# A Softplus burst and a copy moved ahead of a pair of exponentials in a four-layer state-space kernel

## The chip, the cores and the metric

The kernel runs on one core of a Trainium2 chip. The core has five engines that work side by side, each through its own list of instructions in order: PE (matrix products), DVE (vector work), ACT (functions such as the exponential, each set of which needs a table to be loaded), POOL (general vector work) and SP, which here only starts DMA transfers. The metric is the device time of one execution in microseconds (us). Before the change it is 17365.62 us, the median of three runs (17365.36 to 17379.11).

## What is computed

Eight images of 48 x 48 positions and 96 channels go through four layers, each added to its input. Layers 0 and 3 are two-dimensional state-space layers, layer 2 is one along rows and columns, and layer 1 is a small network between an enlargement and a reduction of the image. The heart of layers 0, 2 and 3 is a scan over 2304 positions, for each of four directions, 192 channels and 16 states:

```python
delta = jax.nn.softplus(dts + dt_projs_bias.reshape(K, Din)[None, :, :, None])
...
def step(h, inp):
    u, dl, Bv, Cv = inp
    dA = jnp.exp(dl[..., None] * A)
    h = h * dA + (dl * u)[..., None] * Bv[:, :, None, :]
    y = jnp.einsum('bkdn,bkn->bkd', h, Cv)
    return (h, y)
```

`delta` is the step size, B and C are made from the input by a small matrix product.

## The kernel before

**Tiling.** A direction of an image is cut into five blocks of 480 or 384 positions (`BLKS`). A block has eight slots (`NG`), each holding two states for 96 channels, and two slots make a turn: four turns a block, 640 turns a layer, 1920 in all. The function `scans` runs the loop over turns for all three scan layers. Each turn has three scans on DVE, in three pairs of units of up to 484 columns.

**The work of a turn.** `make_da(t, pair)` (L327) lets ACT write two exponentials into a PSUM tile `ps_da`, of which there are two, so that a pair is made while the scan of another reads its own. `scan(t, pair)` (L335) is the scan on DVE, in place in the tile `dbu`. `make_dbu` (L303) prepares the products (delta u) B of later slots, in part on DVE, in part on POOL; for each slot a table says how many of its three units go to POOL. DVE reads B from PSUM, from a tile `ps_b`, of which there is one; `copy_b` (L284) fills it on ACT. `make_hc` (L341) multiplies by C on POOL, `reduce` (L361, L363) sums over states on PE, and `done` (L758) takes the sum out of PSUM on ACT.

**The order.** There is no automatic scheduler: the order in which the program text gives out instructions is the order on each engine. In a turn, ACT gets `make_da(t, 1)`, `make_da(t, 2)`, `copy_b` for slot at+3, then what `aside(at)` gives out, then `make_da(t+1, 0)`, `copy_b` for slot at+4 and `aside(at+1)`. DVE gets scan 0, products for slot at+2, scan 1, products for slot at+3, scan 2.

**Beside the turns.** `aside` (called twice a turn, once for each slot) takes finished results of the guest out of PSUM (`guest.settle()`; the guest is layer 1, which runs along with layers 0 and 2), starts loads, takes a step of side work such as convolution or normalisation for other images, and runs the steps that are due for a block two ahead (`run(at)`). Those steps, which `stage1` returns with the slot at which each is due, make B, C, delta and delta u of that block: two matrix products, copies, two additions of the bias (L711, due at slots 4 and 5), then `s6`, one Softplus over both halves of the 192 channels (L735, due at slot 6), then `du` on POOL (L503, due at slot 7), and the stores. Slot 6 is the first of the fourth turn of a block. Softplus and the exponential need different tables, so `s6` brings a table load ahead of it and one ahead of the next exponential. The row-and-column layer (`lines`) has its own `stage1`, with no step of this kind.

Of the kernel before, what the change touches and what calls it, by code (L numbers as in the profile page):

```python
# [101 lines left out]
def vss_stack_kernel(ctx: ExitStack, tc: tile.TileContext, i: dict, out: bass.AP):  # L102
# [120 lines left out]
    def scans(dirs, order, restart, on_pool, a, pools, ps, stage1, opening, done, side, tail, ahead=None, guest=None):  # L223
# [29 lines left out]
        def load_dd(b, half):  # L253

            t = pools["dd"].tile([P, 3 * 2 * WMAX], F32, tag="dd", name="dd")
            nc.sync.dma_start(t[:, :6 * b.m], b.dd[half].unsqueeze(1).to_broadcast([32, 4, 6 * b.m]))
            b.got[half] = t[:, :6 * b.m].rearrange("p (g t m) -> p g t m", g=3, t=2)

        def load_bc(t):

            b, slot = blocks[t // NG], t % NG
            sg = ORDER[slot][1]
            other = t - slot + NG - 1 - slot
            n = min(free, key=lambda n: free[n])
            free[n] = other
            r = bufs[n]
            rows4 = b.bcd[8 * sg:8 * sg + 8, :].rearrange("(s w) n -> s (w n)", w=2)
            nc.sync.dma_start(r[:, LEAD:LEAD + 2 * b.n], rows4.unsqueeze(0).to_broadcast([32, 4, 2 * b.n]))

            lo, hi = LEAD - b.at.start, LEAD + b.n  # L270
            bcs[t] = bcs[other] = r[:, lo:hi + b.at.start], r[:, hi:hi + b.n]

        def copy_b(t):

            if t >= NG * len(blocks):
                return
            b, slot = blocks[t // NG], t % NG
            if on_pool.get(slot) == 3:
                return
            if slot == NG // 2 and t - 1 in bps:  # L280
                bps[t] = bps[t - 1]
                return
            bps[t] = ps("b", 1)
            nc.scalar.copy(bps[t][:, :bcs[t][0].shape[1]], bcs[t][0])  # L284

        def units(tile, b, lo, hi):
            return tile[:, lo * b.m:hi * b.m].rearrange("p (u m) -> p u m", m=b.m)

        def make_dbu(t, engine):

            if t >= NG * len(blocks):
                return
            b, slot = blocks[t // NG], t % NG
            if t // 2 not in dbus:
                dbus[t // 2] = rooms[t // 2 % (NG // 2)]
            cut = 3 - on_pool.get(slot, 0)
            lo, hi = (0, cut) if engine is nc.vector else (cut, 3)
            if lo == hi:
                return
            o = units(dbus[t // 2], b, 3 * (slot % 2) + lo, 3 * (slot % 2) + hi)[:, :, b.by]  # L300
            du = b.got[ORDER[slot][0]][:, lo:hi, 1, b.by]
            by = (bps[t] if engine is nc.vector else bcs[t][0])[:, b.by]
            engine.tensor_mul(o, du, by.unsqueeze(1).to_broadcast([P, hi - lo, by.shape[1]]))  # L303
# [13 lines left out]
        def make_da(t, pair):  # L317
            if t >= nt:
                return
            b, q = turns[t]  # L320
            da = ps("da", 2, 1024)
            das[t, pair] = da
            for u in (2 * pair, 2 * pair + 1):
                half, sg = ORDER[2 * q + u // 3]
                ci = half * 12 + sg * 3 + u % 3
                at = (u - 2 * pair) * b.m
                nc.scalar.activation(da[:, at:at + b.m], b.got[half][:, u % 3, 0, :], AF.Exp, scale=a[:, b.k, ci:ci + 1])  # L327

        def scan(t, pair):
            b, q = turns[t]  # L330
            da = das.pop((t, pair))[:, :2 * b.m]
            db = dbus[t][:, 2 * pair * b.m:(2 * pair + 2) * b.m]
            if b.back:
                da, db = da[:, ::-1], db[:, ::-1]
            nc.vector.tensor_tensor_scan(db, da, db, 0.0, ALU.mult, ALU.add)  # L335

        def make_hc(t, sub):
            b, q = turns[t]
            n = b.n
            h = units(dbus[t], b, 3 * sub, 3 * sub + 3)[:, :, b.at]  # L340
            nc.gpsimd.tensor_mul(h, h, bcs.pop(2 * t + sub)[1].unsqueeze(1).to_broadcast([P, 3, n]))  # L341
# [24 lines left out]
            if sub == 1:  # L366
                dbus.pop(t)

        steps = {}

        def plan(b, at):
            b.got = {}
            sources(b, pools)
            for n, step in stage1(b).items():
                steps.setdefault(at + n, []).append(step)

        def run(t):
            for step in steps.pop(t, []):
                step()

        for n, b in enumerate(blocks[:3]):
            plan(b, NG * (n - 2))
        for t in range(-2 * NG - 1, 0):
            run(t)
            for _ in range(2):
                next(ahead, None)
            while tail:
                tail.pop(0)()
            if t == -NG:
                for n in range(4):  # L390
                    load_bc(n)
            if t == 2 - NG:
                for half in range(2):
                    load_dd(blocks[0], half)
# [30 lines left out]
        for t, (b, q) in enumerate(turns):  # L425
            at, nblk = 2 * t, t // (NG // 2)
            if q == 0:
                if nblk + 3 < len(blocks):
                    plan(blocks[nblk + 3], at + NG)
                if b.k == order[0] and b.first:  # L430
                    beside = side(b.job)
            scan(t, 0)
            if t > 0:
                make_hc(t - 1, 1)
            make_dbu(at + 2, nc.vector)
            make_da(t, 1)
            make_dbu(at + 2, nc.gpsimd)
            make_dbu(at + 3, nc.gpsimd)
            if t > 0:
                reduce(t - 1, 0)  # L440
            scan(t, 1)
            make_da(t, 2)
            copy_b(at + 3)
            make_dbu(at + 3, nc.vector)
            if t > 0:
                reduce(t - 1, 1)
            aside(at)
            begin(t + 2)
            make_hc(t, 0)
            make_da(t + 1, 0)  # L450
            scan(t, 2)
            copy_b(at + 4)
            finish(at + 1)
            aside(at + 1)
            if q == NG // 2 - 1 and b.k == order[-1] and b.last:
                for _ in beside:
                    while tail:
                        tail.pop(0)()
# [25 lines left out]
    def sources(b, pools):  # L484
        b.dd = [pools["dr"].tile([32, 6 * b.m], F32, tag=f"dd{half}_{b.n}", name=f"dd{half}") for half in range(2)]
        b.bcd = pools["dr"].tile([2 * NS, b.n], F32, tag=f"bcd_{b.n}", name="bcd")
# [4 lines left out]
    def sizes(b, half):  # L491

        return [b.dds[:, half, n, b.at] for n in range(2)]
# [20 lines left out]
    def ss2d(l, xin, xout, guest=None):  # L514
# [15 lines left out]
        for n in ("in", "xp", "out"):  # L530
            of = i[f"{l}_{n}"]
# [168 lines left out]
        def stage1(b):  # L700
            n = b.n
            u, uall = b.view(us[b.job], dirs[b.k][0]), b.view(uss[b.job], dirs[b.k][0])
            got = {}

            def raw(half):
                got["p"] = ps("s1", 1)
                nc.tensor.matmul(got["p"][:, :n], lhsT=wide("dtw", (2 * b.k + half) * DH), rhs=b.bcl[:, :n],  # L707
                                 start=True, stop=True)

            def biased(half):  # L710
                nc.scalar.activation(sizes(b, half)[0], got["p"][:DH, :n], AF.Identity,  # L711
                                     bias=w[f"{l}_dtb"][:, b.k, half:half + 1])

            def s0():
                got["p"] = ps("s1", 1)
                for half in range(2):
                    nc.tensor.matmul(got["p"][:, :n], lhsT=wide("xp", (2 * b.k + half) * NBC), rhs=uall[:, half],  # L717
                                     start=(half == 0), stop=(half == 1))

            def s1():  # L720
                b.bcl = pools["bcl"]
                nc.scalar.copy(b.bcl[:NBC, :n], got["p"][:NBC, :n])

            def s3():
                nc.sync.dma_start(b.bcd, b.bcl[:2 * NS, :n])
                raw(0)

            def s4():
                make_room(b, pools)
                biased(0)  # L730
                raw(1)

            def s6():
                both = b.dds[:, :, 0, b.at]
                nc.scalar.activation(both, both, AF.Softplus)  # L735

            def du():
                make_du(b, u)

            def store(half):  # L740
                return lambda: store_dd(b, half)

            return {-1: s0, 1: s1, 3: s3, 4: s4, 5: lambda: biased(1), 6: s6, 7: du,
                    NG: store(0), NG + 1: store(1)}

        def so_far(b, half):
# [606 lines left out]
```

## Time and profile before

| | |
|---|---|
| median of three runs | 17365.62 us |
| the profiled execution | 17373.84 us |
| its span, from first to last instruction | 17371.9 us |
| layer 0, scan loop | 115 to 5809 us |
| layer 2, scan loop | 5906 to 11826 us |
| layer 3, scan loop | 11948 to 17345 us |
| mean granted clock of PE | 0.843 of full speed |

The costliest groups of instructions, each with its line, engine, operation, tiles (written <- read), shape, count, then busy time in us and mean length of one in ns, and last the engine's idle time just before them, with what ended most of it:

```profile
L335 DVE TENSOR_TENSOR_SCAN dbu<-ps_da,dbu 128x968 f32<-128x968 f32 (+3 forms) x5760 | 11823.5, 2075 | 814.5 <-ACT ps_da L327 653.1
L341 POOL TENSOR_TENSOR dbu<-dbu,bc 128x1440 f32<-128x1440 f32 (+1 forms) x3840 | 10069.9, 2635 | 1775.7 <-DVE dbu L335 1715.3
L327 ACT ACTIVATE ps_da<-dd,w_l_a 128x484 f32<-128x484 f32 (+3 forms) x11520 | 7423.0, 649 | 2308.3 <-DVE dbu L335 2078.8
L303 DVE TENSOR_TENSOR dbu<-dd,ps_b 128x962 f32<-128x962 f32 (+5 forms) x2880 | 3831.0, 1330 | 286.1 <-ACT ps_b L284 157.3
L284 ACT COPY ps_b<-bc 128x482 f32<-128x482 f32 (+3 forms) x2720 | 1448.8, 533 | 227.1 <-DVE dbu L303 185.3
L327 ACT ACT_TABLE_LOAD x993 | 1274.0, 1283 | 17.5
```

Of Softplus alone there are 320, 1.01 us for a wide block and 0.85 us for a narrow one, each behind a table load of 1.28 us. In a timeline, a row that ends in x4 is four instructions merged; the bracket at the end of a row is idle time of the engine before it, and what ended it.

### The profile page before, as it was taken

The numbers are of one execution on the slowest core, as the hardware profiler recorded it, in microseconds if no ns is written. First come the engines' busy times: TensorE is split into PE (matmuls) and PEld (weight loads), VectorE is DVE, ScalarE is ACT, GpSimd is POOL, SyncE is SP. The second block draws the span as 40 slices with busy tenths as digits, with TensorE's granted clock in tenths as the row PEclk, the third lists the DMA queues.
The fourth block names the chain that finished last, engine by engine and source line by source line (L and its number), as shares of the span: only waits on it lengthen the run. The fifth ranks groups of instructions, "written<-read, shape, count | busy, mean of one in ns | idle before, by whom it ended". The sixth has DMA issues, their size and how long they took to land.

```text
span 17371.9 us, 169003 instructions
## 1 busy us (share of the span) xinstructions
PE 13193.7 (76%) x53740; PEld 4744.7 (27%) x53740; DVE 15807.2 (91%) x9840; ACT 13897.8 (80%) x20972; POOL 15212.7 (88%) x8159
## 2 busy tenths in 40 slices
PE   6778788878787677777777777776777777777776
PEld 1223232323232333233233322221222222222221
DVE  7999999998899789899889999996999999999998
ACT  6888888878787688888888888886878878878876
POOL 7998888988889788888888888887999999999998
PEclk7888888888897888899889988887878878878877
DMA  4555555454545344444444444443455555555454
GB/s 141 178 174 169 176 168 179 167 183 165 173 169 181 130 149 165 149 157 154 156 155 149 159 158 155 150 155 128 171 173 176 174 174 175 174 169 179 169 176 144
DMA packets 887919, 2843.67 MB, mean 164 GB/s; under 512 B 353468, under 2 KB 421788, under 8 KB 760206
## 3 DMA queue, kind: packets, MB, share of 16 engines
q1 hardware_dynamic: 887022, 2832.85, 48.0%
q8 instruction: 423, 6.93, 0.2%
q14 instruction: 474, 3.88, 0.1%
HBM read 2384.40 MB, written 448.17 MB: 163 GB/s over the span
## 4 chain that ended last, share of the span: by engine, by line
ACT 22%; DVE 21%; POOL 19%; issue 14%; PE 13%; DMA 10%; SPq 1%; POOLq 0%; DVEq 0%; ACTq 0%
DVE dbu L335 14%; POOL dbu L341 12%; ACT ps_da L327 8%; DVE dbu L303 6%; POOL dbu L303 4%; DMA dd<-dds 4%; DMA dd<-dd 3%; ACT L327 3%; PE ps_y L361 2%; POOL dds L503 2%; ACT ps_b L284 1%; PE ps_sa L944 1%; PE ps_sa L889 1%; DMA bc<-bcd 1%; ACT L907 1%
## 5 line engine op out<-in xcount | busy, mean ns | idle before, releaser
L335 DVE TENSOR_TENSOR_SCAN dbu<-ps_da,dbu 128x968 f32<-128x968 f32 (+3 forms) x5760 | 11823.5, 2075 | 814.5 <-ACT ps_da L327 653.1
L341 POOL TENSOR_TENSOR dbu<-dbu,bc 128x1440 f32<-128x1440 f32 (+1 forms) x3840 | 10069.9, 2635 | 1775.7 <-DVE dbu L335 1715.3
L327 ACT ACTIVATE ps_da<-dd,w_l_a 128x484 f32<-128x484 f32 (+3 forms) x11520 | 7423.0, 649 | 2308.3 <-DVE dbu L335 2078.8
L361 PE MATMUL ps_y<-dbu,w_red 128*32 128x480 f32 (+1 forms) x23040 | 4206.5, 651 | 1588.0 <-POOL dbu L341 1554.0
L363 PE MATMUL ps_y<-dbu,w_red 128*32 128x480 f32 (+1 forms) x7680 | 4168.0, 651 | 0.0
L303 DVE TENSOR_TENSOR dbu<-dd,ps_b 128x962 f32<-128x962 f32 (+5 forms) x2880 | 3831.0, 1330 | 286.1 <-ACT ps_b L284 157.3
L303 POOL TENSOR_TENSOR dbu<-dd,bc 128x481 f32<-128x481 f32 (+5 forms) x2240 | 3913.5, 1762 | 22.5 <-DMA dd<-dd 18.2
L361 PEld LDWEIGHTS ps_y<-dbu,w_red 128*32 128x32 f32 x23040 | 724.9, 118 | 5000.1 <-POOL dbu L341 3338.6
L284 ACT COPY ps_b<-bc 128x482 f32<-128x482 f32 (+3 forms) x2720 | 1448.8, 533 | 227.1 <-DVE dbu L303 185.3
L578 PE MATMUL ps_side<-xpad,w_l_cw 128*128 128x480 f32 (+1 forms) x2880 | 1360.4, 611 | 46.4 <-ACT g_room L1179 16.3
L327 ACT ACT_TABLE_LOAD x993 | 1274.0, 1283 | 17.5
L707 PE MATMUL ps_s<-bcl,square 128*128 128x480 f32 (+1 forms) x1280 | 890.0, 786 | 324.1 <-ACT dds L711 169.5
L357 PE MATMUL ps_y<-big,eye 128*128 128x480 f32 (+1 forms) x960 | 745.0, 865 | 243.5 <-ACT big L758 238.9
L717 PE MATMUL ps_s<-big,square 128*128 128x480 f32 (+1 forms) x1280 | 844.9, 790 | 66.1 <-ACT g_room L1179 18.4
L503 POOL TENSOR_TENSOR dds<-dds,big 96x960 f32<-96x960 f32 (+1 forms) x320 | 706.7, 2209 | 144.9 <-ACT dds L735 144.6
L578 PEld LDWEIGHTS ps_side<-xpad,w_l_cw 128*128 128x128 f32 x2880 | 575.0, 210 | 815.0 <-issue 703.4
L889 PE MATMUL ps_sa<-ub,square 128*128 128x480 f32 (+1 forms) x640 | 411.7, 782 | 394.2 <-ACT ub L879 394.2
L363 PEld LDWEIGHTS ps_y<-dbu,w_red 128*32 128x32 f32 x7680 | 661.9, 118 | 0.0
L870 PE MATMUL ps_sb<-xpad,square 128*128 128x480 f32 (+1 forms) x1280 | 595.2, 611 | 84.7 <-ACT g_room L1179 32.7
L870 PE MATMUL ps_sa<-xpad,square 128*128 128x480 f32 (+1 forms) x1280 | 537.9, 561 | 0.0
L711 ACT ACTIVATE dds<-ps_s,w_l_dtb 96x480 f32<-96x480 f32 (+1 forms) x640 | 405.1, 633 | 124.6 <-DMA dd<-dds 82.9
L758 ACT COPY big<-ps_y 96x480 f32<-96x480 f32 (+1 forms) x640 | 471.6, 737 | 38.7 <-PE ps_y L363 37.4
(244 smaller groups left out, 12498.7 us busy)
## 6 DMA issues: line engine op xcount, KB each, us to landing
dd<-dd SPq DMA_DIRECT2D x512, 1452.0 KB
bc<-bcd SPq DMA_DIRECT2D x1536, 480.0 KB
dd<-dd SPq DMA_DIRECT2D x256, 1440.0 KB
dd<-dds SPq DMA_DIRECT2D x512, 363.0 KB
dd<-dd SPq DMA_DIRECT2D x128, 1164.0 KB
bc<-bcd SPq DMA_DIRECT2D x384, 384.0 KB
dd<-dds SPq DMA_DIRECT2D x256, 360.0 KB
dd<-dd SPq DMA_DIRECT2D x64, 1152.0 KB
```

The costliest lines, as they stand in the source:

```text
L284: nc.scalar.copy(bps[t][:, :bcs[t][0].shape[1]], bcs[t][0])
L303: engine.tensor_mul(o, du, by.unsqueeze(1).to_broadcast([P, hi - lo, by.shape[1]]))
L327: nc.scalar.activation(da[:, at:at + b.m], b.got[half][:, u % 3, 0, :], AF.Exp, scale=a[:, b.k, ci:ci + 1])
L335: nc.vector.tensor_tensor_scan(db, da, db, 0.0, ALU.mult, ALU.add)
L341: nc.gpsimd.tensor_mul(h, h, bcs.pop(2 * t + sub)[1].unsqueeze(1).to_broadcast([P, 3, n]))
L361: nc.tensor.matmul(y[32 * g:32 * g + 32, :n], lhsT=wc["red"][:, :32], rhs=hc[:, g, b.at], start=False, stop=(slot == 3))
L363: nc.tensor.matmul(y[DH:, :n], lhsT=wc["red"][:, 32:], rhs=hc[:, 2, b.at], start=False, stop=(slot == 3))
L503: nc.gpsimd.tensor_mul(du, dt, u)
L578: nc.tensor.matmul(pu[:, :n], lhsT=flat[:, at:at + P], rhs=xpad[:, r0 + dy:r0 + dy + nr, dx:dx + W], start=(tap == 0), stop=(tap == 8))
L707: nc.tensor.matmul(got["p"][:, :n], lhsT=wide("dtw", (2 * b.k + half) * DH), rhs=b.bcl[:, :n], start=True, stop=True)
L717: nc.tensor.matmul(got["p"][:, :n], lhsT=wide("xp", (2 * b.k + half) * NBC), rhs=uall[:, half], start=(half == 0), stop=(half == 1))
L870: nc.tensor.matmul(got["u", half][:, :n], lhsT=wide("cw", at), rhs=shifted(off), start=(tap == 0), stop=(tap == 3))
```

## The change

Steps that `stage1` gives with a tuple as their slot go into a second list, `bursts`. In layers 0 and 3 this is `s6` alone, the Softplus. In the loop, the burst that is due at slot `at` is given out behind `make_da(t, 1)` and no longer in `aside(at)`, which comes behind `make_da(t, 2)` and the copy of B. Where there is a burst in the turn, `copy_b(at + 3)`, the copy for the odd slot, follows it at once, and so stands ahead of `make_da(t, 2)` too. In the other turns, and in layer 2, the order is as it was.

```diff
-        steps = {}
+        steps, bursts = {}, {}
 
         def plan(b, at):
             b.got = {}
             sources(b, pools)
             for n, step in stage1(b).items():
-                steps.setdefault(at + n, []).append(step)
-
-        def run(t):
-            for step in steps.pop(t, []):
+                if isinstance(n, tuple):
+                    bursts.setdefault(at + n[0], []).append(step)
+                else:
+                    steps.setdefault(at + n, []).append(step)
+
+        def run(t, of=steps):
+            for step in of.pop(t, []):
                 step()
...
         for t in range(-2 * NG - 1, 0):
+            run(t, bursts)
             run(t)
...
             make_dbu(at + 2, nc.vector)
             make_da(t, 1)
+            early = at in bursts
+            run(at, bursts)
+            if early:
+                copy_b(at + 3)
             make_dbu(at + 2, nc.gpsimd)
             make_dbu(at + 3, nc.gpsimd)
             if t > 0:
                 reduce(t - 1, 0)
             scan(t, 1)
             make_da(t, 2)
-            copy_b(at + 3)
+            if not early:
+                copy_b(at + 3)
             make_dbu(at + 3, nc.vector)
...
-            return {-1: s0, 1: s1, 3: s3, 4: s4, 5: lambda: biased(1), 6: s6, 7: du,
+            return {-1: s0, 1: s1, 3: s3, 4: s4, 5: lambda: biased(1), (6,): s6, 7: du,
                     NG: store(0), NG + 1: store(1)}
```

In layer 2's own `stage1` every due slot is a plain number, so nothing of it moves.

## The prediction, made before the result

> **Terms.** A turn handles two of a block's eight slots. In it E0, E1, E2 are the three pairs of exponentials on ACT (L327), S0, S1, S2 the three scans on DVE (L335) that consume them, D the products `make_dbu` (L303) that DVE makes between scans for the next turn. The burst is: load the Softplus table, Softplus (L735), and the load of the Exp table that the next exponential then needs. It stands in the fourth turn of a block; E0' and S0' belong to the turn after it.
>
> **What bounds the kernel now.** I read the busy shares first, then DVE's waits, then two stretches around a burst.
>
> ```profile
> span 17371.9 us, 169003 instructions
> PE 13193.7 (76%) x53740; PEld 4744.7 (27%) x53740; DVE 15807.2 (91%) x9840; ACT 13897.8 (80%) x20972; POOL 15212.7 (88%) x8159
> ```
>
> DVE is idle for 17371.9 - 15807.2 = 1565 us in all, so a change that only moves ACT work can win no more than a part of that. The waits of DVE name the part that ACT causes:
>
> ```profile
> DVE dbu L335 <- ACT ps_da L327: 653.1, 614, 4.5
> DVE dbu L335 <- issue: 94.5, 75, 4.5
> DVE dbu L335 <- POOL dbu L341: 28.3, 17, 1.9
> ```
>
> Scans wait 653 us for exponentials; POOL, though 88% busy, holds scans for 28 us only. The middle layer (5906 to 11826 us) has no L735 at all, so I sorted DVE's idle time in the two outer layers by turn and scan. Before S0', the scan behind a burst, it is 155 us in the first layer and 38 us in the last (158 bursts each); before S2 of the burst's turn it is 0.0 us in both. Those 193 us are all that the change can give back directly, and the zero is what it can spoil.
>
> The timeline of ACT in the last layer (start, length, engine, line, names):
>
> ```profile
> 14234.73 0.56 ACT L711 ACTIVATE dds<-ps_s,w_l_dtb 96x384 f32<-96x384 f32 x1
> 14235.19 2.65 ACT L327 ACTIVATE ps_da<-dd,w_l_a 128x484 f32<-128x484 f32 x4
> 14237.91 0.56 ACT L284 COPY ps_b<-bc 128x482 f32<-128x482 f32 x1
> 14238.50 1.28 ACT L735 ACT_TABLE_LOAD   x1
> 14239.79 0.85 ACT L735 ACTIVATE dds<-dds 96x768 f32<-96x768 f32 x1
> 14240.66 1.28 ACT L327 ACT_TABLE_LOAD   x1
> 14241.95 1.37 ACT L327 ACTIVATE ps_da<-dd,w_l_a 128x484 f32<-128x484 f32 x2
> ```
>
> and of DVE beside it:
>
> ```profile
> 14236.25 1.63 DVE L303 TENSOR_TENSOR dbu<-dd,ps_b 128x1443 f32<-128x1443 f32 x1
> 14237.80 2.16 DVE L335 TENSOR_TENSOR_SCAN dbu<-ps_da,dbu 128x968 f32<-128x968 f32 x1
> 14239.88 1.63 DVE L303 TENSOR_TENSOR dbu<-dd,ps_b 128x1443 f32<-128x1443 f32 x1
> 14241.43 4.23 DVE L335 TENSOR_TENSOR_SCAN dbu<-ps_da,dbu 128x968 f32<-128x968 f32 x2
> ```
>
> The reader should see two things. E1 and E2 are one run of four (x4): nothing on ACT waits between them, so there is no hole there for a burst. And S2 and S0' are one run of two (x2): behind the burst E0' ends at 14243.32, S2 ends about 14243.5, so here the burst is already hidden, narrowly, by S1, D and S2. In the first layer, evictions of the guest layer (L1172, L1190) stand ahead of the burst and the cover is gone:
>
> ```profile
> 2498.90 0.65 ACT L1172 ACTIVATE g_room<-ps_side,g_shift,g_rs 96x365 f32<-96x365 f32 x1
> 2501.30 0.40 ACT L1190 COPY g_room<-ps_s 73x288 f32<-73x288 f32 x1 [1.75 <-PE ps_s L1188]
> 2501.71 1.28 ACT L735 ACT_TABLE_LOAD   x1
> ```
> ```profile
> 2506.57 2.17 DVE L335 TENSOR_TENSOR_SCAN dbu<-ps_da,dbu 128x968 f32<-128x968 f32 x1 [2.79 <-ACT ps_da L327]
> ```
>
> **What the Trainium skill says.** "ScalarE: Activation LUTs", What ACT_TABLE_LOAD costs: a switch of table is a load of about 1283 ns and a drain of about 1380 ns. The trace agrees on the load (1283 ns, all 320 at L735) and not on the drain: the next ACTIVATE starts 0.01 us behind the load. I use 1.28 us. The same page, Table sets, says that copies and Identity are in every set; the trace agrees, L711 and L284 run between exponentials without a load. "Perfetto Trace Analysis", Identifying the Most-Contended Engine, ranks these engines by occupancy: DVE here. Its section on the DVE / Act instruction says that the update of a semaphore travels after the reported end; here S0' starts 0.03 us behind E0' where it waited (2505.17 + 1.37 to 2506.57), which is what I charge for a hand-over.
>
> **The change part by part.**
>
> *Instructions.* Nothing goes but line positions: the order on PE, DVE, POOL and SP is unchanged, and ACT has one table load more in the whole program (no Silu shares the burst's stretch, so no switch is saved or added). Cost of that: 1.3 us.
>
> *The burst ahead of E2.* ACT's order becomes E1, burst, copy of B, E2, evictions, E0'. The copy needs the previous D done, which it is before S1 starts, so it doesn't wait. From the end of E1 to the earliest S2, for the wide blocks: table 1.28, Softplus 1.01, copy 0.55, table 1.28, E2 1.37, gaps 0.08, hand-over 0.03, together 5.60 us. One block in five is narrow (Softplus 0.85, copy 0.47, or E2 1.20), so the mean is near 5.5. What covers it is the way from the end of E1 to S2 on DVE: rest of the wait for S1, S1 itself 2.16, D 1.63. Taken from the trace for the 158 turns of each layer, it is 4.35 us in the mean (median 4.2) in the first layer and 4.78 (median 4.8) in the last. So S2, never late before, becomes late by 5.5 - 4.35 = 1.15, about 1.2 us with the few turns of zero left out, and by 5.5 - 4.78 = 0.7, about 0.8 us. In the stretch above: E1 ends 14236.50, and 14236.50 + 1.28 + 0.85 + 0.56 + 1.28 + 1.37 + 0.11 = 14241.95 against 14241.43.
>
> *The copy put ahead too.* D for the odd slot reads it. It ends 2.88 us behind E1, S1 ends 2.2 to 3.3 us behind it, so D starts at most 0.7 us later, and ends 4.5 us behind E1, ahead of E2's 5.57. Hidden by E2; if E2 were not late this would cost 0.2 us a burst. Had the copy stayed behind E2, D would have started at 5.6 and S2 at 7.2.
>
> *The stall that goes.* ACT reaches E0' with the same work done, so E0' ends about when it did. S0' is then released by S2's end. Given back: 155 / 158 = 0.97 us a burst in the first layer, 38.5 / 158 = 0.24 in the last. What is late next is S2 itself, whose delay runs through to S0'.
>
> *Sum.* Last layer: 0.8 - 0.24 = +0.56 us, x 158 = +88 us. First layer: 1.2 - 0.97 = +0.23 us if E0' never is the later one. But in 100 of the 158 turns guest evictions stand between E2 and E0', and where such an eviction waits for PE, whose matmul waits for an eviction in front of it (the 1.75 us above), that wait moves along with E2 and E0' stays late; if it does in all, the net is +0.5. I take the middle, +0.37 x 158 = +58 us. In the turn behind, ACT has a little more room: the scans S1 there wait for ACT 16 + 5 us today, of which I take off 15. Together 88 + 58 - 15 + 1 = +132 us.
>
> *Does it stay?* ACT meets DVE again within two turns (in turn 1 of a block E0 waits for a scan in 132 and 156 of 156 blocks), so DVE's delay isn't won back there. POOL starts its second product of the burst's turn 1.65 us (median) behind S2 anyway, so S2's delay hardly reaches it. Softplus ends earlier, but its reader on POOL (L503) waits 31 us for it in the first layer and nothing in the last: nothing to win. SP's loads are far off.
>
> Against the profiled execution's 17373.84 us (8.2 above the median of 17365.62) this is 17506; against the median, **17497 us**, 0.8% slower.
>
> **Rivals.**
> 1. *Faster: the burst is hidden.* S2 isn't delayed because the cover is really as long as the burst, and S0' loses its stall. Speaks for it: S0' has the only systematic stall. Against: cover 4.35 and 4.78 against 5.5; only some 10% of turns have 5.6 or more. It decides if the chain behind E1 takes under 4.3 us in fact. It would give 17366 - 193 + 15 = about 17190; half of it, 17280.
> 2. *No change: exchange.* One stall for another of the same size, in the last layer taken up by waits for PE and POOL later on. For: both layers do the same work on ACT. Against: the last layer has only 38 us to give. 17366 +- 35.
> 3. *Slower by more.* Guest evictions come 3.5 us later against E1, so PE's next guest matmuls and the evictions behind them push E0' and the next turn's E1 as well, beyond the 1.2 us of room there (in the second stretch E1 of that turn ends at 2508.53, its S1 starts at 2509.71). At 0.5 us more for the 100 guest turns and the full +0.5 in the first layer: 132 + 50 + 21, and S2 late by another 0.1 in both, +32: about 17600.
> 4. *The text does not do what it says.* Excluded: all bursts of the loop are taken at E1, one per block.
>
> **How the numbers follow.** Forecast (17400 to 17570) 0.70, rival 3 (17570 and up) 0.12, rival 2 0.09, rival 1 0.09. Measurement can't tell changes under 0.2%, 35 us. The ends of the unknown sizes, first layer +0.1 to +0.5 and last +0.4 to +0.7, give +64 to +190, and with rival 3 the range is 17400 to 17590. Faster 0.09, within 0.2% 0.09, slower 0.82.
>
> **What would show it.** In the profile after, S2 of the burst's turn should wait for E2 (idle about 185 us in the first layer, 125 in the last), S0' should hardly wait in the last layer, DVE's wait for L327 should rise from 653 to about 653 + 310 - 137 = 826 us (137 is L327's share of the 193), and the table loads stay at 1283 ns. The forecast is wrong if S2 waits for under 0.4 us in the mean, or if DVE's idle time falls elsewhere.

## The result, and the profile after

The changed kernel takes 17445.32 us (median of 6 runs, 17421.44 to 17448.41), the kernel before 17368.66 us in the same comparison (6 runs, 17365.36 to 17384.28). The ratio is 1.0039, with a 95% interval of 1.0026 to 1.0052: about 77 us slower, where 132 us were forecast.

In the code after the change the lines of the steps are higher by 9: Softplus is L744 for L735, the bias L720 for L711, the guest's evictions L1181, L1188 and L1199 for L1172, L1179 and L1190. The busy time of each engine in the changed kernel:

```profile
PE 13221.8 (76%) x53740; PEld 4769.1 (27%) x53740; DVE 15826.8 (91%) x9840; ACT 13880.1 (80%) x20973; POOL 15217.0 (87%) x8159
```

No engine has more instructions of the kernel to do, but for one table load more on ACT. DVE's waits in the changed kernel, as who waited for whom, us in total, times, longest:

```profile
DVE dbu L335 <- ACT ps_da L327: 737.4, 800, 4.4
DVE dbu L303 <- ACT ps_b L284: 210.8, 106, 76.8
```

Scans waited for exponentials 614 times for 653 us before, now 800 times for 737 us: more often, and for less each time. The second line is new in the loops: before, a product D waited for its copy of B 6 times for 157 us (153 of them in two waits at the start of layers 0 and 3), now 106 times for 211 us.

The same turn of layer 3 that was shown before, on DVE and then on ACT (start, length, engine, line, operation, tiles, shape, count):

```profile
14289.60 2.16 DVE L335 TENSOR_TENSOR_SCAN dbu<-ps_da,dbu 128x968 f32<-128x968 f32 x1
14291.68 1.63 DVE L303 TENSOR_TENSOR dbu<-dd,ps_b 128x1443 f32<-128x1443 f32 x1
14293.68 4.24 DVE L335 TENSOR_TENSOR_SCAN dbu<-ps_da,dbu 128x968 f32<-128x968 f32 x2 [0.37 <-ACT ps_da L327]
```
```profile
14286.98 1.36 ACT L327 ACTIVATE ps_da<-dd,w_l_a 128x484 f32<-128x484 f32 x2
14288.36 1.28 ACT L744 ACT_TABLE_LOAD   x1
14289.66 0.85 ACT L744 ACTIVATE dds<-dds 96x768 f32<-96x768 f32 x1
14290.41 0.55 ACT L284 COPY ps_b<-bc 128x482 f32<-128x482 f32 x1
14290.98 1.28 ACT L327 ACT_TABLE_LOAD   x1
14292.27 2.66 ACT L327 ACTIVATE ps_da<-dd,w_l_a 128x484 f32<-128x484 f32 x4
```

The run of four exponentials is cut: E1 alone, then the burst and the copy, and then E2 and E0' as a new run of four. S2 now waits 0.37 us for E2; before, S2 followed D with no wait. S0' follows S2 at once, as it did before. So this turn only lost.

The turn of layer 0 that had a stall of 2.79 us at S0', on DVE and ACT after the change (two rows of ACT are left out):

```profile
2516.72 4.29 DVE L335 TENSOR_TENSOR_SCAN dbu<-ps_da,dbu 128x968 f32<-128x968 f32 x2 [0.82 <-ACT ps_da L327]
```
```profile
2515.32 1.37 ACT L327 ACTIVATE ps_da<-dd,w_l_a 128x484 f32<-128x484 f32 x2
2517.16 0.38 ACT L1199 COPY g_room<-ps_s 73x288 f32<-73x288 f32 x1
2517.44 1.37 ACT L327 ACTIVATE ps_da<-dd,w_l_a 128x484 f32<-128x484 f32 x2
2520.44 0.32 ACT L1199 COPY g_room<-ps_side 73x192 f32<-73x192 f32 x1 [1.15 <-PE ps_side L1197]
```

Here the change does what it can do: the stall of 2.79 us is gone, for one of 0.82 us at S2. The first eviction L1199 starts without a wait; its twin before the change waited 1.75 us for PE. But the second one, behind E0', now waits 1.15 us, ahead of the next turn's E1. Before the change it had no wait:

```profile
2506.96 0.31 ACT L1190 COPY g_room<-ps_side 73x192 f32<-73x192 f32 x1
```

Over all turns with a burst, taken from the two traces (157 turns a layer, means in us):

| | layer 0 before | after | layer 3 before | after |
|---|---|---|---|---|
| end of E1 to start of S2 | 4.34 | 5.49 | 4.76 | 5.49 |
| end of S2 to start of S0' | 1.23 | 0.20 | 0.47 | 0.16 |
| start of S1 to start of S0' | 6.95 | 7.09 | 6.17 | 6.59 |
| start of S1 to S1 of the next turn | 10.09 | 10.31 | 9.21 | 9.61 |
| from block to block | 35.51 | 35.75 | 33.62 | 33.84 |
| the layer's loop of scans | 5693.3 | 5736.9 | 5396.3 | 5429.0 |

The loops of layers 0 and 3 grew by 43.6 and 32.7 us; that of layer 2, in which nothing moved, shrank by 5.3 us. (It lies between 5898 and 5920 us in the profiles of all kernels here that leave layer 2 alone; what differs by 10 us in one layer of one profile is not told apart from that.)

### The profile page after: what moved, and what is told of

It is laid out like the page before. It is cut to its first block, busy times and chain, and to the rows that moved or that the text cites. A ratio compares the mean times of both kernels' runs of the same rounds, so it can differ in the third digit from the quotient of the medians.

```text
span 17443.4 us, 169089 instructions
## 1 busy us (share of the span) xinstructions
PE 13221.8 (76%) x53740; PEld 4769.1 (27%) x53740; DVE 15826.8 (91%) x9840; ACT 13880.1 (80%) x20973; POOL 15217.0 (87%) x8159
## 4 chain that ended last, share of the span: by engine, by line
ACT 24%; DVE 21%; POOL 15%; issue 14%; PE 13%; DMA 10%; SPq 1%; POOLq 0%; DVEq 0%; ACTq 0%
DVE dbu L335 14%; POOL dbu L341 9%; ACT ps_da L327 8%; DVE dbu L303 6%; DMA dd<-dds 4%; POOL dbu L303 4%; ACT L327 3%; DMA dd<-dd 3%; PE ps_y L361 2%; POOL dds L512 2%; ACT ps_b L284 2%; PE ps_sa L898 1%; DMA bc<-bcd 1%; PE ps_sa L953 1%; ACT L744 1%
## 5 line engine op out<-in xcount | busy, mean ns | idle before, releaser
L303 DVE TENSOR_TENSOR dbu<-dd,ps_b 128x962 f32<-128x962 f32 (+5 forms) x2880 | 3833.9, 1331 | 324.3 <-ACT ps_b L284 210.8
L303 POOL TENSOR_TENSOR dbu<-dd,bc 128x481 f32<-128x481 f32 (+5 forms) x2240 | 3913.9, 1762 | 22.4 <-DMA dd<-dd 18.8
L720 ACT ACTIVATE dds<-ps_s,w_l_dtb 96x480 f32<-96x480 f32 (+1 forms) x640 | 404.7, 632 | 108.7 <-DMA dd<-dds 69.3
```

## The experiments

Times before, in the same comparisons, are 17374.45 us for the first four, 17372.88 for the next three, 17369.63 for the last.

**One layer at a time.** The burst's slot is a tuple in one of the two layers only:

```diff
-            return {..., (6,): s6, 7: du,
+            return {..., (6,) if l == "l0" else 6: s6, 7: du,
```

> The new order in layer 0 only; layer 3 keeps the old one. Cover theory (the chain from the end of E1 over burst and copy to E2 is longer than what DVE has to do before S2; S2's delay less the stall given back at S0' is the loss): 158 x (1.14 - 1.00) = +22 us at the bursts, with what follows about +20 to +45 us. Rival (the loss comes about elsewhere, by guest evictions and PE that are later): all of the +77 us are here, since only this layer has a guest beside its bursts.

> The new order in layer 3 only. Cover theory: S2 later by 0.72 us, 0.31 given back at S0', 158 x 0.41 = +65 us, or the +33 us by which this layer's loop grew in the changed kernel if later waits for POOL and PE take part of it back. Rival (the loss is the guest's): 0 +- 15 us, there is no guest in this layer.

Layer 0 alone: 17407.73 us, ratio 1.0020 (1.0013 to 1.0027), +33 us. Layer 3 alone: 17410.02 us, 1.0019 (1.0012 to 1.0026), +36 us. Together that is +69 us against +77: the loss is in both layers and adds up. The guest can't be the cause of layer 3's half, since it isn't there. In layer 3 the +36 us are well under the +65 that the delay at S0' alone would give, so about half is taken back later.

Where it is taken back shows when the time from each scan to the next is summed over layer 3's loop, before and after the change. The way from S1 to S2 in the burst's turn grows by 113 us, that from S2 to S0' shrinks by 47, which leaves 66. Then the three turns between two bursts are shorter by 9, 13 and 9 us. With the change in layer 3 alone they are shorter by 8, 13 and 8 us, and with it in layer 0 alone none of them changes by much over 2 us. DVE's waits for POOL in layer 3's loop seem to name a cause. In the kernel before they are:

```profile
DVE dbu L335 <- POOL dbu L341: 21.3, 12, 1.9
DVE dbu L303 <- POOL dbu L315: 13.1, 10, 1.5
```

and all that is left of them in the changed one:

```profile
DVE dbu L303 <- POOL dbu L315: 1.0, 1, 1.0
```

But only the second group is gone: the product L303 in the second turn of a block waits 13 us for POOL before and 1.6 us after (waits too short for this view counted in), and that turn's 13 us are nearly all from there. The first group, scans of narrow blocks, still waits, under another name. One of these scans with its exponentials, before and after:

```profile
12467.37 1.21 ACT L327 ACTIVATE ps_da<-dd,w_l_a 128x388 f32<-128x388 f32 x2
12468.67 1.77 DVE L335 TENSOR_TENSOR_SCAN dbu<-ps_da,dbu 128x776 f32<-128x776 f32 x1 [1.84 <-POOL dbu L341]
```
```profile
12509.30 1.21 ACT L327 ACTIVATE ps_da<-dd,w_l_a 128x388 f32<-128x388 f32 x2
12510.60 1.77 DVE L335 TENSOR_TENSOR_SCAN dbu<-ps_da,dbu 128x776 f32<-128x776 f32 x1 [1.83 <-issue]
```

Both start 0.09 us behind the end of their exponentials, so both wait for ACT, and neither for what the bracket says. The same holds for all 14 such scans: 25.6 us before (21.3 put down to POOL, 4.3 to "issue"), 24.6 us after, all put down to "issue". So POOL accounts for 11 of the 31 us taken back; the rest are small waits, 7 us of them waits of the burst turn's own S0 for its exponentials. That DVE's delay is what makes these waits shorter is argued, not shown. It fits the next two experiments, in which layer 3's S0' is later still and the three turns together are shorter by 34 and 42 us.

**The burst moved, the copy left behind E2.**

```diff
             make_da(t, 1)
             early = at in bursts
             run(at, bursts)
-            if early:
-                copy_b(at + 3)
...
             make_da(t, 2)
-            if not early:
-                copy_b(at + 3)
+            copy_b(at + 3)
```

> Burst behind E1 as in the change, the copy of B back behind E2. Cover theory: the product D waits for the copy and S2 for D, so the chain from E1 is table 1.28, Softplus 1.0, table 1.28, E2 1.35, copy 0.53, D 1.6, about 7.1 us, against a cover of 4.35 and 4.78: S2 late by 2.7 and 2.3 us, less 1.0 and 0.3 given back, 158 x (1.7 + 2.0) = about +580 us over before. Rival (the copy was hidden either way, its move does nothing): +77 us like the change.

Measured: 17871.87 us, ratio 1.0284 (1.0269 to 1.0299), +497 us. The rival falls. S2 comes 7.10 and 7.08 us behind E1's end (expected about 7.1). In the profile of this kernel, layer 3's turn:

```profile
14592.15 1.66 DVE L303 TENSOR_TENSOR dbu<-dd,ps_b 128x1443 f32<-128x1443 f32 x1 [1.95 <-ACT ps_b L284]
14593.72 4.23 DVE L335 TENSOR_TENSOR_SCAN dbu<-ps_da,dbu 128x968 f32<-128x968 f32 x2
```
```profile
14590.26 1.37 ACT L327 ACTIVATE ps_da<-dd,w_l_a 128x484 f32<-128x484 f32 x2
14591.57 0.54 ACT L284 COPY ps_b<-bc 128x482 f32<-128x482 f32 x1
```

E2 is ready at 14591.63, but S2 can't use it: D stands ahead of S2 on DVE and waits for the copy until 14592.15. The move of the copy is the half of the change that keeps it cheap. Of the 83 us between 580 and 497, about 25 are missing at S0' already, which is late by 1.62 and 1.89 us in the mean (555 us in all); most of the rest is again recovered later, since a block is longer by 1.53 and 1.66 us.

**The copy ahead of the burst.** The two are exchanged:

```diff
             early = at in bursts
-            run(at, bursts)
             if early:
                 copy_b(at + 3)
+            run(at, bursts)
```

> E1, copy, burst, E2: the copy ahead of the burst and not behind it. Cover theory: the copy has one PSUM tile and waits until DVE has read the last one, which is when S1 starts, 0.7 us (layer 0) and 1.15 us (layer 3) behind E1's end; the burst filled that wait and no longer does. S2 later by that: 158 x (0.7 + 1.15) = +290 us over the change, +370 us over before. Rival (same work between E1 and E2, so the same time; D no longer waits for the copy): +77 us or a little under.

Measured: 17718.95 us, ratio 1.0197 (1.0182 to 1.0213), +344 us. From the end of E1 to S2 it is 6.24 and 6.81 us, 0.75 and 1.32 more than in the change. ACT in the profile of this kernel, the turn of layer 3:

```profile
14449.33 1.36 ACT L327 ACTIVATE ps_da<-dd,w_l_a 128x484 f32<-128x484 f32 x2
14452.05 0.57 ACT L284 COPY ps_b<-bc 128x482 f32<-128x482 f32 x1 [1.36 <-DVE dbu L303]
14452.63 1.28 ACT L744 ACT_TABLE_LOAD   x1
```

The copy starts 1.36 us late here (0.74 us in the mean in layer 0, 1.29 in layer 3), because there is one tile `ps_b` and DVE still reads it. In the change the burst runs through that wait. So the order of the same work between E1 and E2 makes a difference of 270 us.

**A burst without its tables.** The change, with the exponential for Softplus, so that the step size is not a Softplus:

```diff
-                nc.scalar.activation(both, both, AF.Softplus)
+                nc.scalar.activation(both, both, AF.Exp)
```

> The change, with the exponential in place of Softplus in the burst (the step size is left out as a Softplus), so that neither table load is needed there: the chain from E1's end to S2 is 0.98 + 0.53 + 1.33 + 0.1 = about 2.95 us. Cover theory: that is under the cover (mean 4.35 and 4.78 us, 5% of turns under 3.3), so S2 waits no longer (260 us of idle go) and S0' doesn't either: the time falls below the one before by the 137 to 193 us of stall at S0', to about 17190. Rival (it is the change of order and not the length of the chain that costs, by guest evictions, PE and POOL that are later): above the one before, by some 50 us.

Measured: 17255.76 us, ratio 0.9934 (0.9920 to 0.9948), -117 us. In the same position, with 2.91 and 3.09 us from the end of E1 to the end of E2, S2 never waits and keeps its 4.39 and 4.76 us behind E1. So it is the length of the chain that decides whether S2 waits, and not the position by itself. The loops of layers 0 and 3 are 76 and 27 us shorter in the profile (and layer 2's, where nothing moved, 15). That is less than the stall at S0', since waits grew elsewhere: ahead of S1 of the next turn in layer 0 from 18 to 56 us, and ahead of S1 in the second turn of a block in layer 3 from 15 to 30 us. One more rival falls here. In the change the Softplus, and POOL's product that reads it, can come earlier, and that might be what shortens layer 3's other turns; here the function ends earlier still, and the second turn of layer 3's blocks is 22 us longer, not shorter.

**The burst behind E2, ahead of the evictions.** The old place but for the guest; the difference is shown against the changed kernel:

```diff
             make_da(t, 1)
-            early = at in bursts
-            run(at, bursts)
-            if early:
-                copy_b(at + 3)
...
             make_da(t, 2)
-            if not early:
-                copy_b(at + 3)
+            copy_b(at + 3)
+            run(at, bursts)
```

> E2 and the copy where they were before the change, then the burst, and the guest's evictions behind it, then E0'. S2 keeps its cover. Theory (in layer 0 ACT waits 41 us for PE in evictions ahead of the burst; the burst fills that): S0' stalls 30 to 40 us less, 17335, the S2 stall stays 0. Rival (evictions 3.6 us later hold PE and the next evictions back, and E1 of the next turn): no gain, 17374 or above, and DVE waits more at S1 of the next turn.

Measured: 17356.84 us (13 runs), ratio 0.9990 (0.9982 to 0.9998). That is faster than both kernels, by little: 16 us below the one before. The stall at S0' in layer 0 falls from 155 to 120 us, as the theory had it, but DVE waits 15 us more ahead of S1 of the next turn, as the rival had it, and the layer's loop is 4 us shorter in this one profile. Layer 2, in which nothing moved, is 10 us shorter in the same profile, so where the 16 us come from isn't shown.

**E0' ahead of the evictions as well.** Against the kernel just above:

```diff
+            early = at in bursts
             run(at, bursts)
+            if early:
+                make_da(t + 1, 0)
...
-            make_da(t + 1, 0)
+            if not early:
+                make_da(t + 1, 0)
```

> As the one before it, and E0' too ahead of the evictions: E2, copy, burst, E0', evictions. Theory: E0' ends 2.3 us behind the start of S2 in layer 0, S2 takes 2.1 to 2.4 us with what is between: of the 155 us of stall at S0' in layer 0 some 110 to 135 go, in layer 3, with no evictions, nothing changes: 17240 to 17265. Rival (evictions late): DVE's wait at S1 of the next turn rises from 18 us by 50 or more, gain under 60 us.

Measured: 17417.47 us, ratio 1.0026 (1.0016 to 1.0037), +45 us. The theory falls and the rival holds. The stall at S0' in layer 0 falls from 155 to 74 us, but DVE's wait ahead of S1 of the next turn rises from 18 to 84 us, and its waits for PE in that layer from 73 to 120 us. Two rows of ACT in the profile of this kernel, E0' in the turn of layer 0 and an eviction behind it:

```profile
2509.39 1.37 ACT L327 ACTIVATE ps_da<-dd,w_l_a 128x484 f32<-128x484 f32 x2
2513.21 0.31 ACT L1199 COPY g_room<-ps_side 73x192 f32<-73x192 f32 x1 [1.12 <-PE ps_side L1197]
```

The evictions free PSUM for the next matmuls of the guest. Done later, they let PE start later, and the next eviction waits 1.12 us, now ahead of the next E1. Over all these turns, ACT's waits for PE between E0' and the next E1 rise from 16 us in the kernel before to 121 us.

**The guest rests ahead of the burst.** The old order; no step of the guest is given out beside slot 5 in layer 0 (layer 3 has no guest), and a little more beside the turns of layer 2 (there `restart` is true):

```diff
-            if guest:
+            if guest and (restart or slot != 5):
                 guest.turn(slot, clear)
...
-        guest.rate = 0.42
+        guest.rate = 0.55
```

> The old order; the guest gives out nothing beside slot 5 of layer 0, so that no eviction of it stands ahead of the burst in slot 6; its rate in layer 2 is 0.55 in place of 0.42, so that it still ends in time. Theory (of the 155 us of stall at S0' in layer 0, 135 are in the 100 turns with an eviction ahead of the burst, 20 in the 58 without): S0' waits about 158 x 0.34 = 54 us, layer 0's loop is shorter by about 100 us, 5595; layer 2's loop may grow by some tens of us with the guest's work moved there. Rival (the evictions only come elsewhere and delay other scans as much): layer 0's loop 5693 +- 20, DVE's idle time only moved.

Measured: 17333.09 us, ratio 0.9978 (0.9970 to 0.9987): 37 us faster than the kernel before, the fastest of those that keep the Softplus. Layer 0's loop is 5622.6 us, 71 shorter; layer 2's is 5957.2, 37 longer, more than the 22 us by which it differs among the kernels that leave it alone. The stall at S0' in layer 0 falls from 155 to 75 us (54 expected), and DVE's idle time in that layer from 476 to 408 us. So within layer 0 the idle time is gone and not only moved, but about half of the gain is paid for in layer 2, to which the guest's work went.

## Why the prediction was right, and what it mis-sized

*The direction and the mechanism.* The chain from E1 to S2 was put at a mean of 5.5 us against a cover of 4.35 and 4.78; S2 starts 5.49 us behind E1 in both layers, and the chain itself, up to the end of E2, is 5.39 and 5.38 (in about a tenth of the turns DVE's own work is the longer one). S2's delay, forecast as 1.15 to 1.2 and 0.7 to 0.8 us, is 1.15 and 0.73. The exponential in the burst's place, which shortens the chain below the cover, takes the wait away: shown.

*DVE's idle time at S2.* 185 and 125 us were forecast. It is 162 and 99 us with the waits of D for its copy counted in (45 and 9 us of them). The delay was right; the idle time is smaller, as it has to be when DVE's back-to-back instructions overlap by 0.08 us in these traces (S1 runs from 14289.60 to 14291.76, D starts at 14291.68): a wait takes that overlap's place before it shows as idle. All of DVE's waits for exponentials were forecast at 826 us and are 737; 54 of the missing 89 us stand as D's waits for the copy instead.

*The copy.* That D's wait for it is hidden behind E2 fits: S2 comes 5.49 us behind E1, and 7.1 us when the copy stays behind E2. Exchanging copy and burst removes D's wait and makes S2 later, not earlier.

*The stall that goes.* The wait of S0' itself, 155 and 38 us, is 6 and 0 us. (In layer 0 the profile puts 113 of the 155 us down to the exponentials and the rest to other releasers or to none; but every one of these waits ends 0.03 to 0.10 us behind the end of E0'.) The doubt about guest evictions came out at its lower end: in layer 0 ACT waited 41 us for PE between E2 and E0' before, and waits 2 us now. That wait doesn't move along with E2 and E0', as was feared; part of it has moved behind E0', where ACT's waits for PE ahead of the next E1 rose from 16 to 63 us. So the net at S0' is +0.14 us, where +0.37 was taken (the low end was put at +0.23): 22 us, not 58.

*The turn behind.* 15 us were taken off for ACT having more room at S1 of the next turn in layer 0. The opposite came: DVE's idle time before that S1 rose from 18 to 31 us. Evictions come later, and what follows them with PE does too; the experiment that moves E0' shows the same in a stronger form. These two errors, 58 - 22 and 15 + 13, nearly cancel, and the few us that are left come from the turns behind: the layer's loop grew by 43.6 us, against 43 forecast. That this layer came out so close is luck.

*Does it stay?* This is the step that failed. It said that DVE's delay isn't won back. In layer 3, S0' is later by 0.42 us a burst (66 us, 88 forecast), but a block is longer by 0.22 us only, and the loop by 33 us: half of the delay is won back in the three turns between two bursts. The prediction looked for this at the exponentials, at POOL's products behind S2 and at the reader of Softplus, and didn't count DVE's short waits in the other turns. Its reading that POOL holds scans for 28 us goes by the name in the bracket; in layer 3, 21 us of these are waits for exponentials too, and they stayed. The 11 us of the product that waited for POOL are the largest piece; for the rest no one cause is shown. The other part of the error in this layer lies at the burst: S2's delay is 0.73 us where 0.8 was taken, and 0.31 us is given back at S0' where 0.24 was. Of the 55 us between 88 and 33, 22 are of this kind and 33 were won back, and layer 3 makes up the whole difference between +132 and +77 us.

*The rivals.* "Faster" is out: the cover is as short as it was read. "Exchange" is out for the whole, by the interval, but half right for layer 3: part of the loss there is taken up by waits later on, only little of it by waits for POOL. "Slower by more" for the guest's sake came with the change only as the 13 us ahead of S1; with E0' moved as well it outweighs what S0' gains.

## What to carry to other kernels

When a burst is moved ahead of something, add up the chain from the last instruction that must be done to the next one that is waited for, and set it against what the consumer has to do in that time; here 5.5 us against 4.3 to 4.8 us, means over the turns of each layer, told the sign and the size of S2's delay before any run. Then look for waits that are there in the same order: a burst costs least where its engine would stand still (ahead of a single-buffered copy, ahead of an eviction that waits for PE), and exchanging two neighbours (270 us here) can matter more than moving both (77 us). And a delay of the bounding engine doesn't always add to the end: count where it waits for others in the same loop, since a delay can take the place of such a wait. When counting, don't go by the name in the bracket alone: see whether the input that comes last, here the exponentials, ends just before the wait does.

## What was not expected of the hardware

That a new wait costs more than its idle time says: the 0.08 us by which neighbours on DVE overlap in the trace is lost as well. In the changed kernel DVE's busy time, which counts overlapped time once, is 15826.8 us against 15807.2 with the same 9840 instructions; in the loops of layers 0 and 3 the waits of over 0.06 us rose from 604 to 827. 223 times 0.08 us is 18 us, about the 20 us by which the busy time grew. The ten kernels of this document agree: from the one with the fewest such waits in the whole execution (1137, a burst without its tables) to the one with the most (1462, the change) the busy time rises from 15793.8 to 15826.8 us, and the straight line through all ten has 0.09 us a wait.
